# Turning attention weights inside SBUF instead of by way of HBM, in a two-layer attention kernel

## The chip, the cores and the metric

The kernel runs on one core of one Trainium2 chip. The metric is device time in microseconds of that core; the number quoted for a kernel is the median of its runs. A profile is one further execution, recorded instruction by instruction.

## The reference

Two layers of the same shape work on four images of 32 x 32 positions (S = 1024 tokens) with 768 channels. Each layer normalises over 32 groups of channels, runs 12-head attention with head size 64 and decomposed relative position biases, projects the result and adds it to its input. Cut to what matters:

```python
def attention(x, Wqkv, Wproj, bproj, Rh, Rw):          # x: [B, S, 768], after group norm
    q, k, v = split_heads(x @ Wqkv)                     # each [B*12, S, 64]
    rel_h = einsum('bhwc,hkc->bhwk', q.reshape(B*12, 32, 32, 64), Rh)
    rel_w = einsum('bhwc,wkc->bhwk', q.reshape(B*12, 32, 32, 64), Rw)
    bias = (rel_h[..., :, None] + rel_w[..., None, :]).reshape(B*12, S, S)
    attn = softmax(scale * q @ k.T + bias)              # [B*12, S, S]
    return merge_heads(attn @ v) @ Wproj + bproj

x = x + attention(group_norm(x), layer 0)
x = x + attention(group_norm(x), layer 1)               # with a bias on q, k and v
```

All arithmetic is in fp32. The largest piece of data is `attn`: 1024 x 1024 weights for each of 12 heads, 4 images and 2 layers.

## The kernel before

**Units.** Layer and image give eight passes (`images`), each of six head pairs, so there are 48 pairs, numbered `g`; `pair` is the number within its image. A pair is worked through in eight units `n` = 0 to 7 of 128 queries each. The main loop (L566) goes over the 384 units. Scheduling is manual: each engine runs its instructions in the order in which the program writes them.

**Work of a unit**, with the name of the PSUM or SBUF tile that the profile shows. While the loop is at unit n, it issues ahead:
- `biases` (L312) for the unit after next: GpSimd adds the two position terms into `sc` (two instructions, one per head).
- `scores` (L326) for the next unit: TensorE makes `s` = q k (L333; two heads side by side on the upper and lower 64 rows of the array, 512 columns at a time); VectorE adds bias and finds the row extremum in one pass (L342); ScalarE takes the exponential in place (L346). The two banks `s`, one per head, are all that there is: the scores of the next unit need the reductions of this one to be over.
- `turn` (L359) for this unit: VectorE transposes 32 x 32 blocks of the exponentials from `sc` into `tb` (L370).
- `divide` (L351) for the next unit: VectorE's reciprocal (L353), then GpSimd's scaling of `sc` (L356).
- A share of `todo`: the pieces in which TensorE prepares the next pair and projects earlier pairs out. `shares` says how many steps each unit takes.

**Steps of todo.** For the next pair: q in two halves and k in two halves (`project_in`, tile `pj`, L214), six steps each; ScalarE copies half of the contraction out of PSUM (L227 or L229) and VectorE adds the other half (L230). Then two groups of values (`project_values`, tile `pv`, L249), six steps each, with copies by ScalarE and additions by VectorE. From the fourth pair on, also four groups of output projection (`project_out`, tile `o`, L475), three steps each, evacuated by VectorE. `take` runs them in this order. A step of 512 columns costs TensorE 0.86 us: two heads or contraction halves beside each other.

**The tables of positions.** `positions(g, i)` multiplies q by the position tables (tile `tp`, L281); ScalarE copies the result out and sends it to HBM (`tdr`). After both halves `diagonals` (L295) reads it back skewed, with 16 small DMAs on SP's queue, into `rel`. They are put into the lists `early`, `mid` and `later`. In each unit `early` is run and then swapped with `later`: a thing put into `later` runs two units on; one put into `early` after the swap runs one unit on.

**The path of the weights to the value product.** The product needs keys on partitions, the exponentials have queries on partitions. The 32 x 32 block transposes leave each block in its partition group; what is left is a movement of data between partitions. Two units make a quarter of 256 queries. After the second, for each head, SP writes `tb` to HBM (`td`, L373, 1 MiB) and, one or two units later, reads it back in another order into `pt` (`read_back`, L381, 1 MiB). The lists `behind` and `behind2` hold the read until then.

**The value product.** `weigh` (L388) multiplies two quarters by the values into `av` (L399), 256 columns per instruction, two heads in the left and right 64 columns of the array; VectorE copies `av` into `attn` (L408, or L411 with the bias of layer 1). It runs at the end of unit 6 for quarters 0 and 1, and at the end of unit 2 of the next pair for quarters 2 and 3. The last pair's two quarters are done one by one after the loop.

**PSUM**: two tiles of two banks for `s`, two for everything else (`ps_m`).

Of the kernel before, what the change touches and what calls it, by code (L numbers as in the profile page):

```python
# [31 lines left out]
FP = mybir.dt.float32  # L32
# [4 lines left out]
P = 128  # L37
B, HW, C = 4, 32, 768
S = HW * HW
NH, D = 12, 64  # L40
NC = C // P
NT = S // P
# [3 lines left out]
HALF = 512  # L46
LAYERS = 2
NP = NH // 2
# [6 lines left out]
def attention_blocks(ctx: ExitStack, tc: tile.TileContext, a: dict, out: bass.AP):  # L55
    nc = tc.nc
# [8 lines left out]
    vpool = ctx.enter_context(tc.tile_pool(name="v", bufs=3))  # L65
    scpool = ctx.enter_context(tc.tile_pool(name="sc", bufs=6))
    tmppool = ctx.enter_context(tc.tile_pool(name="tmp", bufs=1))
    tbpool = ctx.enter_context(tc.tile_pool(name="tb", bufs=3))
    ptpool = ctx.enter_context(tc.tile_pool(name="pt", bufs=2))
    relpool = ctx.enter_context(tc.tile_pool(name="rel", bufs=2))  # L70
    iopool = ctx.enter_context(tc.tile_pool(name="io", bufs=4))
    small = ctx.enter_context(tc.tile_pool(name="small", bufs=4))
# [11 lines left out]
    NPAIR = NI * NP  # L84
# [33 lines left out]
    for l in range(LAYERS):  # L118
        tab = const.tile([P, 2, 2 * HW], FP, tag=f"tab{l}", name=f"tab{l}")
        nc.gpsimd.memset(tab, 0.0)  # L120
        for i, ax in enumerate("hw"):
            src = a[f"rel{ax}{l}"]
            n = src.shape[1]
# [78 lines left out]
    def project_in(g, which, i):  # L202

        im, pair = divmod(g, NP)
        xn, w = xn_of[im], w_of[g, which]
        cols = slice(i * HALF, (i + 1) * HALF)
        if i == 0:
            tag = "qk"[which]
            qk_of[g, which] = qkpool.tile([P, S], FP, tag=tag, name=f"{tag}_{g}")
        t = ps_m.tile([P, 2, HALF], FP, tag="m", name=f"pj_{g}_{which}_{i}")  # L210
        for c in range(NC):
            for a in range(2):
                rows = slice(a * D, (a + 1) * D)
                nc.tensor.matmul(  # L214
                    t[:, a, :], lhsT=w[rows, c, :], rhs=xn[c][rows, cols],
                    start=(c == 0), stop=(c == NC - 1),
                )
            if c < NC - 1:
                yield True
        to, t = qk_of[g, which], [t[:, a, :] for a in range(2)]  # L220
        if which == 1:
            to = to.rearrange("p (a m) -> p a m", a=4)[:, :, i * P : (i + 1) * P]
            t = [x.rearrange("p (m a) -> p a m", a=4) for x in t]
        else:
            to = to[:, cols]
        if images[im][0] == 0:
            nc.scalar.copy(to, t[0])  # L227
        else:
            nc.scalar.activation(to, t[0], AF.Identity, bias=bqkv[:, which, pair : pair + 1])  # L229
        nc.vector.tensor_tensor(to, t[1], to, ALU.add)  # L230
        if which == 0:
            (later if g else mid).append(lambda: positions(g, i))
        if i == 1 and g + 1 < NPAIR:
            later.append(lambda: load_w(g + 1, which))
        yield True
# [121 lines left out]

    def turn(g, n):

        quarter, j = divmod(n, 2)
        for h in range(2):
            if j == 0:
                tb_of[h] = tbpool.tile([P, HW, 2, HW], FP, tag="tb", name=f"tb_{g}_{n}_{h}")
            tb = tb_of[h]
            nc.vector.transpose(tb[:, :, j, :], sc_of[g, n, h])  # L370
            if j == 1:
                td = dram2.tile([P, S * 2], FP, tag=f"td{h}", name=f"td_{g}_{n}_{h}")
                nc.sync.dma_start(out=td, in_=tb.rearrange("p k n i -> p (k n i)"))  # L373
                (behind if quarter % 2 else behind2).append(
                    lambda queue=None, h=h, td=td: read_back(g, quarter, h, td, queue)
                )

    def read_back(g, quarter, h, td, queue=None):
        pt = ptpool.tile([P, 4, NT, 2 * HW], FP, tag=f"pt{h}", name=f"pt_{g}_{quarter}_{h}")
        pt_of[g, quarter, h] = pt  # L380
        (queue or nc.sync).dma_start(  # L381
            out=pt.rearrange("p r k t -> p r (k t)"),
            in_=td.rearrange("(r j) (a t) -> (j a) r t", r=4, a=4),
        )

    def weigh(g, quarters):

        if quarters[0] == 0:
            attn_of[g] = apool.tile([P, S], FP, tag="attn", name=f"attn_{g}")
        n = len(quarters)
        av = ps_m.tile([P, S], FP, tag="m", name=f"av_{g}_{quarters[0]}")[:, : n * 2 * P]
        for at, quarter in enumerate(quarters):
            for k in range(NT):
                for h in range(2):
                    rows = slice(h * D, (h + 1) * D)
                    nc.tensor.matmul(  # L399
                        av[rows, at * 2 * P : (at + 1) * 2 * P], lhsT=v_of[g][:, k, rows],  # L400
                        rhs=pt_of[g, quarter, h][:, :, k, :], start=(k == 0), stop=(k == NT - 1),
                    )
        at = quarters[0] * 2 * P
        to = attn_of[g][:, at : at + n * 2 * P].rearrange("p (q n r i) -> p q r n i", q=n, n=2, r=4)
        av = av.rearrange("p (q r n i) -> p q r n i", q=n, n=2, r=4)
        im, pair = divmod(g, NP)
        if images[im][0] == 0:
            nc.vector.tensor_copy(to, av)  # L408
        else:
            for q in range(n):  # L410
                nc.vector.tensor_scalar(to[:, q], av[:, q], bqkv[:, 2, pair : pair + 1], None, ALU.add)  # L411

    def cuts(im):
        return [0, NC // 2, NC] if im + 1 < NI else [0, NC // 2, NC - 1, NC]
# [86 lines left out]

    early, mid, later, behind, behind2 = [], [], [], [], []

    def run(todo):
        while todo:  # L510
            todo.pop(0)()
# [30 lines left out]
    with tc.manual_schedule(engines=ENGINES):  # L542
# [23 lines left out]
        for at, (g, n) in enumerate(units):  # L566
            im, pair = divmod(g, NP)
            end = im + 1 == NI
            if n == 0:
                shares = [6, 6, 0, 6, 12, 6, 0, 12]  # L570
                ins = (todo if at == 0 else []) + prepare(g + 1)
                if pair < 3:
                    if at == 0:
                        shares = [12, 6, 0, 6, 12, 6, 0, 0]
                    todo = ins + (put_out(im - 1, 1, range(4 * pair, 4 * pair + 4)) if im else [])
                elif pair < NP - 1:
                    todo = ins + put_out(im, 0, range(4 * pair - 12, 4 * pair - 8))
                    if pair == 3 and not end:
                        stages, apply = norm(im + 1)
                else:  # L580
                    todo = ins + put_out(im, 0, range(8, 12))
                    if end:
                        fetch_last()
                        todo += put_out(im, 1, range(12)) + put_out(im, 2, range(0, 12, 2))
                        shares = [6, 6, 0, 6, 6, 2, 0, 4]
            if (pair, n) in loads and not end:
                load_x(im + 1, loads[pair, n])
            if im + 1 < B:
                if (pair, n) in loads0:
                    load_x(im + 1, loads0[pair, n], loads0[pair, n] + AHEAD)  # L590
                if pair < 3 and n in (1, 3, 5, 6):
                    c, i = divmod(4 * pair + n // 2, 2)
                    x = xn_of[im + 1][c % AHEAD][:, i * HALF : (i + 1) * HALF]
                    later.append(lambda c=c, i=i, x=x: stats(im + 1, (c + AHEAD) % NC, i, x))
            run(early)
            early, later = later, early
            if at + 2 < len(units):
                biases(*units[at + 2])
            if at + 1 < len(units):
                scores(*units[at + 1])  # L600
            run(behind)
            behind, behind2 = behind2, behind
            if pair == 3 and n in stages and not end:
                stages[n]()
            if pair == 4 and n in (2, 4, 6) and not end:
                apply(n // 2 - 1)
            share = shares[n]
            first = 3 if n == NT - 1 else 2 if end and pair == NP - 1 and n in (3, 4) else 0
            first = min(first, share)
            take(todo, first)  # L610
            share -= first
            turn(g, n)
            if at + 1 < len(units):
                divide(*units[at + 1])
            if pair == 4 and n == 7 and not end:
                for chunks in ((3, 4), (5,)):
                    take(todo, 3)
                    share -= 3
                    for c in chunks:
                        apply(c)  # L620
            take(todo, share)
            if n == 6:
                weigh(g, (0, 1))
            elif n == 2 and g:
                weigh(g - 1, (2, 3))
        for read in behind:
            read(nc.scalar)
        take(todo, 12)
        for quarter in (2, 3):
            weigh(NPAIR - 1, (quarter,))  # L630
        todo = put_out(NI - 1, 2, range(1, 12, 2))
        take(todo, len(todo))

# [54 lines left out]
```

## Time and profile before

| | us |
|---|---|
| median of 3 runs | 3504.99 (3502.89 to 3509.22) |
| span of the profiled execution | 3507.0 |
| ScalarE: exponentials L346, 768 | 879.8, of 1147 ns each |
| VectorE: score reductions L342, 768 | 909.8, of 1222 ns |
| VectorE: block transposes L370, 768 | 910.7, of 1222 ns |
| GpSimd: biases L319, 768 | 1890.4, of 2485 ns |
| GpSimd: divisions L356, 768 | 855.1, of 1127 ns |
| TensorE: av L399, 6144 records | 689.1, of 382 ns |
| DMA: 624,857 packets | 1084.54 MB, mean 309 GB/s |
| DMA: td<-tb, 384 of 1 MiB | 5.9 from issue to landing (median) |
| DMA: pt<-td, 384 of 1 MiB | 7.6 from issue to landing (median; those of SP) |

The span is first instruction to last in the profiled execution, 2.0 us above the median of the runs and within their spread. A TensorE instruction in fp32 makes two records, and two instructions on different parts of the array run beside each other; records last longer than the steps between them, since their ends are modelled. So TensorE time is best read as the distance from one group's start to the next one's. The granted TensorE clock is 0.998 on average, with short stretches at half speed at the start, near 123, 133 and 198 us, and at the end. DMA queue q1 (SP) takes 83.4% of the DMA engines' time, q10 (ScalarE) 4.4%.

### The profile page before, as it was taken

Reading aid. Unit: us, or ns where it says so; the run is one execution under the profiler, and the core shown is the slowest. Engines: PE = TensorE matmul, PEld = TensorE weight load, DVE = VectorE, ACT = ScalarE, POOL = GpSimd, SP = SyncE. Lnnn points to the kernel's source line nnn. Section 1 sums busy time; section 2 is a strip of 40 time slices with the busy share of each in tenths; the row PEclk is TensorE's granted clock in tenths of the full one; section 3 lists DMA queues with packets and bytes.
Section 4 is the critical chain, followed back from the end, with each engine's and each line's share of the span. In section 5 each row is a group of like instructions: output and inputs, shape, how many; then the busy total and the mean of one; then the engine's idle time right before and its main releaser. Section 6 shows DMA issues by size and latency. Waiting matters only on the chain.

```text
span 3507.0 us, 55102 instructions
## 1 busy us (share of the span) xinstructions
PE 3462.3 (99%) x21120; PEld 1921.4 (55%) x21120; DVE 2381.1 (68%) x3676; ACT 1227.5 (35%) x2040; POOL 2729.9 (78%) x1546
## 2 busy tenths in 40 slices
PE   6999999999999999999999999999999999999999
PEld 4555555555555555555555555555555555555554
DVE  4666767767677676767767667666666667666666
ACT  2334333333333333333333333333333333333331
POOL 3888887778777787788777788787787778787774
PEclk9999999999999999999999999999999999999999
DMA  4889989999899898898989989899889988898877
GB/s 137 312 308 311 332 293 337 319 316 326 304 329 323 313 316 313 312 324 305 326 305 326 320 292 332 311 331 306 300 327 324 321 298 316 319 322 295 311 275 281
DMA packets 624857, 1084.54 MB, mean 309 GB/s; under 512 B 247120, under 2 KB 310096, under 8 KB 575440
## 3 DMA queue, kind: packets, MB, share of 16 engines
q1 hardware_dynamic: 569008, 1028.29, 83.4%
q10 hardware_dynamic: 55584, 52.72, 4.4%
q8 instruction: 166, 2.72, 0.3%
q14 instruction: 99, 0.81, 0.1%
HBM read 580.59 MB, written 500.27 MB: 308 GB/s over the span
## 4 chain that ended last, share of the span: by engine, by line
PE 97%; DMA 2%; DVE 0%; SPq 0%; issue 0%; ACT 0%; POOL 0%; ACTq 0%; DVEq 0%
PE pj L214 28%; PE s L333 19%; PE av L399 19%; PE o L475 14%; PE pv L249 14%; PE tp L281 3%; DMA tdr<-t 1%; DMA pt<-td 1%; SPq L307 0%; DMA td<-tb 0%; DMA wo<-in_wo 0%; DMA xn<-in_x 0%; DVE st L152 0%; DMA rel<-tdr 0%; DMA per<-mv 0%
## 5 line engine op out<-in xcount | busy, mean ns | idle before, releaser
L319 POOL TENSOR_TENSOR sc<-rel 128x1024 f32<-128x1024 f32 x768 | 1890.4, 2485 | 38.2 <-DMA rel<-tdr 38.2
L356 POOL TENSOR_SCALAR sc<-sc,sm 128x1024 f32<-128x1024 f32 x768 | 855.1, 1127 | 686.1 <-DVE sm L353 669.2
L346 ACT ACTIVATE sc<-sc,sm 128x1024 f32<-128x1024 f32 x768 | 879.8, 1147 | 1370.9 <-DVE sm L342 1368.7
L342 DVE CUSTOM_DVE_ANT_0 sc<-s,sc 128x1024 f32<-128x1024 f32 x768 | 909.8, 1222 | 293.3 <-PE s L333 266.4
L214 PE MATMUL pj<-xn,w 64*128 64x512 f32 x4608 | 1033.5, 591 | 26.8 <-DVE xn L193 25.7
L370 DVE STREAM_TRANSPOSE tb<-sc 128x1024 f32<-128x1024 f32 x768 | 910.7, 1222 | 22.9 <-DMA td<-tb 20.5
L214 PEld LDWEIGHTS pj<-xn,w 64*128 64x128 f32 x4608 | 453.2, 188 | 568.6 <-issue 536.6
L333 PE MATMUL s<-k,q 64*128 64x512 f32 x3072 | 750.1, 598 | 7.0 <-DVE sm L342 6.9
L399 PE MATMUL av<-pt,v 128*64 128x256 f32 x6144 | 689.1, 382 | 6.1 <-DMA pt<-td 6.1
L399 PEld LDWEIGHTS av<-pt,v 128*64 128x64 f32 x6144 | 434.5, 137 | 289.8 <-ACT v L259 35.6
L249 PE MATMUL pv<-wv,xn 64*128 64x256 f32 x4608 | 515.7, 376 | 0.0
L249 PEld LDWEIGHTS pv<-wv,xn 64*128 64x128 f32 x4608 | 448.3, 187 | 90.8 <-issue 30.1
L475 PE MATMUL o<-attn,wo 128*128 128x512 f32 x1080 | 475.8, 597 | 0.2 <-DMA wo<-in_wo 0.2
L333 PEld LDWEIGHTS s<-k,q 64*128 64x128 f32 x3072 | 288.5, 187 | 299.5 <-issue 275.5
L475 PEld LDWEIGHTS o<-attn,wo 128*128 128x128 f32 x1080 | 201.4, 190 | 271.4 <-issue 260.9
L260 DVE TENSOR_TENSOR v<-pv,v 128x256 f32<-128x256 f32 x192 | 81.5, 425 | 277.6 <-ACT v L259 277.6
L259 ACT COPY v<-pv 128x256 f32<-128x256 f32 x192 | 71.5, 372 | 330.7 <-PE pv L249 282.9
L286 ACT COPY t<-tp 128x1024 f32<-128x1024 f32 x96 | 97.2, 1012 | 245.5 <-PE tp L281 148.5
L346 ACT ACTIVATION_READ_ACCUMULATOR sc<-sc,sm 128x1 f32 x768 | 143.6, 187 | 0.0
L230 DVE TENSOR_TENSOR q<-pj,q 128x512 f32<-128x512 f32 x96 | 66.4, 692 | 107.5 <-ACT q L227 56.0
L230 DVE TENSOR_TENSOR k<-pj,k 128x512 f32<-128x512 f32 x96 | 66.4, 692 | 95.5 <-ACT k L227 49.0
L281 PEld LDWEIGHTS tp<-tab,q 64*128 64x128 f32 x1536 | 100.0, 187 | 39.9 <-issue 39.6
(34 smaller groups left out, 787.6 us busy)
## 6 DMA issues: line engine op xcount, KB each, us to landing
td<-tb SPq DMA_DIRECT2D x384, 1024.0 KB, 5.9
pt<-td SPq DMA_DIRECT2D x382, 1024.0 KB, 7.6
tdr<-t ACTq DMA_DIRECT2D x96, 512.0 KB, 6.3
w<-in_wqk SPq DMA_DIRECT2D x96, 384.0 KB, 7.5
rel<-tdr SPq DMA_DIRECT2D x760, 32.0 KB, 2.3
part<-res SPq DMA_DIRECT2D x84, 256.0 KB, 5.5
res<-part SPq DMA_DIRECT2D x84, 256.0 KB, 9.1
wv<-in_wv SPq DMA_DIRECT2D x24, 768.0 KB, 8.7
```

Of the source, the lines that this page charges most:

```text
L214: nc.tensor.matmul(t[:, a, :], lhsT=w[rows, c, :], rhs=xn[c][rows, cols], start=(c == 0), stop=(c == NC - 1),)
L230: nc.vector.tensor_tensor(to, t[1], to, ALU.add)
L249: nc.tensor.matmul(t[:, a, k, :], lhsT=xn[c][rows, (2 * i + k) * P : (2 * i + k + 1) * P], rhs=w[rows, c, :], start=(c == 0), stop=(c == N ...
L281: nc.tensor.matmul(ps[:, h, j, :], lhsT=q[rows, at * P : (at + 1) * P], rhs=tabs[l][rows, :], start=True, stop=True,)
L319: nc.gpsimd.tensor_tensor(sc.rearrange("p (a k) (u l) -> p a (k u) l", a=4, l=8), rel[:, h, 0, n, :].unsqueeze(1).unsqueeze(3).to_broadcas ...
L333: nc.tensor.matmul(ps[h][:, cols], lhsT=q[rows, n * P : (n + 1) * P], rhs=k[rows, cols], start=True, stop=True,)
L342: nc.vector.tensor_tensor_reduce(out=sc, in0=ps[h], in1=sc, scale=-scale, scalar=BIG, op0=ALU.add, op1=ALU.min, accum_out=st[:, 0, h : h + 1],
L346: nc.scalar.activation(sc, sc, AF.Exp, bias=st[:, 0, h : h + 1], scale=-1.0, accum_out=st[:, 1, h : h + 1],)
L356: nc.gpsimd.tensor_scalar(sc, sc, st[:, 2, h : h + 1], 1.0, ALU.mult, ALU.mult)
L370: nc.vector.transpose(tb[:, :, j, :], sc_of[g, n, h])
L399: nc.tensor.matmul(av[rows, at * 2 * P : (at + 1) * 2 * P], lhsT=v_of[g][:, k, rows], rhs=pt_of[g, quarter, h][:, :, k, :], start=(k == 0) ...
L475: nc.tensor.matmul(t, lhsT=wo_of[im, o, c], rhs=attn_of[im * NP + c][:, cols], start=(c == c0), stop=(c == c1 - 1),)
```

## The change

The weights no longer go through HBM. A block b is again 256 queries (two units), but both heads now share one `tb` tile of 2 MiB, and `move` copies it straight into `pt` with 16 DMAs of 128 KiB: for each of the four residues `a` of the destination partitions and each group `r` of 32 source partitions. DMAs with r = 0 and 2 are issued on SP, those with r = 1 and 3 on ScalarE. `move` is run in the unit after the block's second one, after that unit's `scores` are issued, so on ScalarE behind their exponentials. One `pt` tile holds two blocks of both heads, with one buffer; `tb` has two.

`weigh` takes a half (512 queries) at once with 512 columns per instruction. It runs at the end of unit 5 and of unit 1 of the next pair. The shares of `todo` change with it, `positions` of q's first half run one unit earlier, and the list `behind2` is gone. After the loop the last block is moved, what is left of `todo` is done and then the last half is weighed. [...]

```diff
-    tbpool = ctx.enter_context(tc.tile_pool(name="tb", bufs=3))
-    ptpool = ctx.enter_context(tc.tile_pool(name="pt", bufs=2))
+    tbpool = ctx.enter_context(tc.tile_pool(name="tb", bufs=2))
+    ptpool = ctx.enter_context(tc.tile_pool(name="pt", bufs=1))
...
-            (later if g else mid).append(lambda: positions(g, i))
+            (mid if not g else later if i else early).append(lambda: positions(g, i))
...
+        b, j = divmod(n, 2)
+        if j == 0:
+            tb_of[b] = tbpool.tile([P, HW, 2, 2, HW], FP, tag="tb", name=f"tb_{g}_{b}")
+        tb = tb_of[b]
         for h in range(2):
-            if j == 0:
-                tb_of[h] = tbpool.tile([P, HW, 2, HW], FP, tag="tb", name=f"tb_{g}_{n}_{h}")
-            tb = tb_of[h]
-            nc.vector.transpose(tb[:, :, j, :], sc_of[g, n, h])
-            if j == 1:
-                td = dram2.tile([P, S * 2], FP, tag=f"td{h}", name=f"td_{g}_{n}_{h}")
-                nc.sync.dma_start(out=td, in_=tb.rearrange("p k n i -> p (k n i)"))
-                (behind if quarter % 2 else behind2).append(
-                    lambda queue=None, h=h, td=td: read_back(g, quarter, h, td, queue)
+            nc.vector.transpose(tb[:, :, h, j, :], sc_of[g, n, h])
+        if j == 1:
+            behind.append(lambda: move(g, b, tb))
+
+    def move(g, b, tb):
+        half, u = divmod(b, 2)
+        if u == 0:
+            pt_of[g, half] = ptpool.tile(
+                [P, 2, 4, NT * 4 * HW], FP, tag="pt", name=f"pt_{g}_{half}"
+            )
+        pt = pt_of[g, half].rearrange("(j a) u r x -> a j u r x", a=4)
+        src = tb.rearrange("p (a k) h n i -> p a (k h n i)", a=4)
+        for a in range(4):
+            for r in (0, 2, 1, 3):
+                (nc.scalar if r % 2 else nc.sync).dma_start(out=pt[a][:, u, r, :], in_=src[r * HW : (r + 1) * HW, a, :])
+
+    def weigh(g, half):
...
+        for k in range(NT):
+            for h in range(2):
+                rows = slice(h * D, (h + 1) * D)
+                nc.tensor.matmul(
+                    av[rows, :], lhsT=v_of[g][:, k, rows], rhs=pt[:, :, k, h, :],
+                    start=(k == 0), stop=(k == NT - 1),
                 )
...
             if n == 0:
-                shares = [6, 6, 0, 6, 12, 6, 0, 12]
+                shares = [12, 0, 6, 6, 12, 0, 6, 6]
...
                     if at == 0:
-                        shares = [12, 6, 0, 6, 12, 6, 0, 0]
+                        shares = [12, 6, 6, 6, 12, 0, 0, 0]
...
-                        shares = [6, 6, 0, 6, 6, 2, 0, 4]
+                        shares = [6, 0, 6, 5, 4, 0, 5, 2]
...
             run(behind)
-            behind, behind2 = behind2, behind
...
-            first = 3 if n == NT - 1 else 2 if end and pair == NP - 1 and n in (3, 4) else 0
+            first = 0 if n < 6 else 2 if end and pair == NP - 1 else 3
...
-            if n == 6:
-                weigh(g, (0, 1))
-            elif n == 2 and g:
-                weigh(g - 1, (2, 3))
-        for read in behind:
-            read(nc.scalar)
-        take(todo, 12)
-        for quarter in (2, 3):
-            weigh(NPAIR - 1, (quarter,))
+            if n == 5:
+                weigh(g, 0)
+            elif n == 1 and g:
+                weigh(g - 1, 1)
+        run(behind)
+        take(todo, len(todo) * NC)
+        weigh(NPAIR - 1, 1)
...
-    nc = bacc.Bacc("TRN2", target_bir_lowering=False, num_devices=1)
+    nc = bacc.Bacc("TRN2", target_bir_lowering=False, num_devices=1, dynamic_dma_scratch_size=1024)
```

## The prediction

> **What bounds the kernel now.** I read four views: the page's busy times and chain, the waits of TensorE, its timeline over one head pair in mid-run, then ACT and SP at the start, where they show what a DMA issue costs.
>
> ```profile
> PE 3462.3 (99%) x21120; PEld 1921.4 (55%) x21120; DVE 2381.1 (68%) x3676; ACT 1227.5 (35%) x2040; POOL 2729.9 (78%) x1546
> ...
> PE 97%; DMA 2%; DVE 0%; SPq 0%; issue 0%; ACT 0%; POOL 0%; ACTq 0%; DVEq 0%
> ```
>
> TensorE sets the time: 3462.3 of 3507.0 us busy, and the chain is TensorE throughout. DMA is on it for 2%, though the DMA engines are 88% busy: halving their traffic buys nothing by itself.
>
> ```profile
> PE s L333 <- DVE sm L342: 6.9, 6, 1.4
> PE av L399 <- DMA pt<-td: 6.1, 3, 3.0
> ```
>
> Apart from the 25.7 us start these are the only waits of weight, and asking for 270 to 3415 us alone lists none: nothing to win in mid-run by an earlier arrival. Where the named ones lie:
>
> ```profile
> 119.04 0.65 PE L399 MATMUL av<-pt,v 128*64 128x256 f32 x2 [0.74 <-DMA pt<-td]
> 122.66 5.35 PE L399 MATMUL av<-pt,v 128*64 128x256 f32 x30 [2.98 <-DMA pt<-td]
> 127.94 1.99 PE L333 MATMUL s<-k,q 64*128 64x512 f32 x8
> 131.36 3.45 PE L333 MATMUL s<-k,q 64*128 64x512 f32 x7 [1.43 <-DVE sm L342]
> ...
> 3491.42 5.35 PE L399 MATMUL av<-pt,v 128*64 128x256 f32 x30 [2.40 <-DMA pt<-td]
> ```
>
> The first value product, the seams of the first three pairs (131, 197, 262 us), and the last product. Now the timeline, start against start:
>
> ```profile
> 1508.66 5.32 PE L214 MATMUL pj<-xn,w 64*128 64x512 f32 x24
> 1513.81 1.88 PE L333 MATMUL s<-k,q 64*128 64x512 f32 x8
> 1515.53 5.32 PE L214 MATMUL pj<-xn,w 64*128 64x512 f32 x24
> 1520.68 5.35 PE L249 MATMUL pv<-wv,xn 64*128 64x256 f32 x48
> 1525.86 1.88 PE L333 MATMUL s<-k,q 64*128 64x512 f32 x8
> ...
> 1532.76 1.88 PE L333 MATMUL s<-k,q 64*128 64x512 f32 x8
> 1534.57 7.13 PE L399 MATMUL av<-pt,v 128*64 128x256 f32 x64
> 1541.62 1.99 PE L333 MATMUL s<-k,q 64*128 64x512 f32 x8
> 1543.54 10.57 PE L475 MATMUL o<-attn,wo 128*128 128x512 f32 x24
> 1554.04 1.99 PE L333 MATMUL s<-k,q 64*128 64x512 f32 x8
> 1555.86 5.32 PE L214 MATMUL pj<-xn,w 64*128 64x512 f32 x24
> ```
>
> Scores (s) take 1.72 us between projections, 1.81 ahead of av, 1.92 between av and o, 1.82 after o: each change of array shape (64x128, 128x64, 128x128) costs 0.1 us in the scores, and more inside the visiting group.
>
> [...] (two 512-column passes in 5.15/12 = 0.4292 us, two 256-column ones in 5.18/24 = 0.2158). [...] every new copy reads 32 partitions.
>
> **Part by part.** A pair's eight units are n = 0 to 7; Tn is the start of unit n's scores or tables on TensorE.
>
> *Wider products.* A half costs 16 x 0.4292 instead of 32 x 0.2158 us: 0.04 less, 96 halves: -3.8 us. The switches (7.05 - 6.91 = 0.14 inside) stay.
>
> *Shares.* Value products move from n = 2 and 6 to n = 1 and 5, with the same neighbours. But the four output groups of a pair, 12 steps together in n = 7, become 6 in n = 6 and 6 in n = 7 with scores between: one more visit to the 128x128 shape. Price: 0.1 into it, 10.50 - 24 x 0.4292 = 0.20 inside, 0.1 after: 0.40 us. Pairs 3 to 46: 44 x 0.40 = +17.5 us.
>
> *First three pairs* have no output groups, so n = 6 and 7 hold scores alone, where before it was n = 7. Scores then run at VectorE's pace: reductions 2.3, transposes 2.4, reciprocal 0.1, with GpSimd's 7.1 per unit behind. Following unit by unit: s(7) ends 10.6 us after T5, its reductions at 13.2, transposes and reciprocal at 15.6, the next reductions at 18.0, the scores after them at 19.9, against 14.1 for a TensorE that never waits. Loss 5.8; before, some 2.4 (1.43 of wait and the serial halves around it). 3 x 3.4 = +10 us.
>
> *First and last product.* DMAs of two units earlier have landed by then (rel issues end near 100 us, the copies near 108, the product comes near 112), so 0.74 + 2.98 go, and 2.0 of half clock behind them (30 matmuls in 5.28 instead of 3.24): -5.7. At the end, 14 steps (12 us) cover the last copies: -2.4, -1.7 of half clock, +0.5 since both bias additions (0.88) stand before the last outputs: -3.6.
>
> *Copies.* 768 transfers of 1 MiB (805 MB) become 3,072 of 128 KiB (403 MB): -402 MB, worth nothing here. The cost is where they are issued. In units 0, 2, 4 and 6 ACT issues eight directly behind its exponentials, and its copies out of PSUM queue behind them. Nearest row:
>
> ```profile
> 50.53 4.54 ACTq L307 DMA_DIRECT2D rel<-tdr x8
> 55.11 0.59 ACT L227 COPY k<-pj 128x512 f32<-128x512 f32 x1 [7.54 <-DMA rel<-tdr]
> ```
>
> Eight on ACT beside eight on SP: 4.54 us, and the k copy waits. Also
>
> ```profile
> SPq L124 <- DMA xn<-in_x: 5.3, 3, 2.2
> ```
>
> in SP's own waits: tables of positions wait for inputs with which they share no data, so DMAs must wait for the landing of one some eight back. That holds the fifth copy of each engine until the first has landed (2.0 to 3.2 us for those eight). I take 4.8 us per eight, since each carries four times the bytes; bounds 4.2 and 6.
>
> Unit 2 is the tight one. Exponentials end at T2 + 6.65 (tables 1.0, then 5.65 as at 1506.94 to 1512.6), copies are issued until 11.45. The k projection is done at 7.86, so its PSUM copy is 3.6 us late; copy and addition take 1.3 (1514.03 to 1515.33), behind which VectorE has the reductions of n = 4's scores (2.3 + 0.1). They end at T2 + 15.15, plus 0.14 to TensorE, 15.3. The scores of unit 4 want that bank at T4 = T2 + 7.86 + 6.87 = 14.73. TensorE waits 0.57. In unit 4 the exponentials then end near T4 + 7.0, the copies are issued by 11.8 and landed by 14.1 (2.3 each); the product comes at 13.9 plus the 0.57 lost. That just fits. Units 0 and 6 have room: q after 12 us, o without ACT. I take 0.6 us for 47 pairs: +28 us. Bounds: 0 with a block of 4.2 us; 3 us per pair (+140) with 6, where the landing misses the product too.
>
> On SP eight copies follow the 16 rel loads (0.5 to 0.67 each) and end before ACT's. Tables one unit earlier: cost nothing, hidden by TensorE. Fewer tb and pt buffers: a tb half has two units, pt is free once the product ahead of the scores is done: nothing.
>
> **Sum.** -3.8 + 17.5 + 10 - 5.7 - 3.6 + 28 = +42 us on the span of 3507.0. The span stands 2.0 above the median of 3504.99 and inside its runs (3502.89 to 3509.22), so the median goes to about 3546 us.
>
> **Rivals.**
> 1. *The ACT block stays hidden* (block under 4.3 us): no stall in unit 4; +14, 3519 us. For it: ACT is 35% busy and SBUF copies need no HBM read. Against: 0.1 us of margin.
> 2. *Copies land late*: [...] block 6 us, landing after T4 + 15; +90 to +160, around 3620 us. For it: [...] 0.9 us of room in unit 5. [...]
> 3. *Faster*, one mechanism: the output groups' second visit turns out free[...]. Then -3.8 - 5.7 - 3.6 = -13 meets only the first pairs' +10; with that stall also under 4 us the result is 3496 or below. It decides once split and stalls together cost less than 6 us. Against: 0.1 us at each of four kinds of border, the same to 0.01 us throughout mid-run.
> 4. *No change*: split half as dear and no stall, +5, 3510 us.
>
> **Chances.** Forecast (+22 to +90) 0.45, rival 1 (+8 to +22) 0.30, rival 2 0.15, rival 4 0.06, rival 3 0.04. A change under 0.2% (7 us) can't be told from none. So faster 0.04, same 0.06, slower 0.90. Range 3513 to 3605: it leaves out rivals 3 and 4 and the worse half of rival 2.
>
> **What would show it.** In the timeline: two o groups of 12 with scores between, 5.35 each; av 7.02 us instead of 7.05; waits of PE s on DVE sm once per pair near 0.6 us, in the unit behind k's first half; ACT's k copy 3 to 4 us behind its projection; av waiting on tb copies in few or no pairs; no pt wait near 120 and 3491 us; seams of about 6 us in the first three pairs. An average wait over 1.5 us per pair, or one below 0.1, would make the size wrong; an unchanged 10.5 us o group, or a faster kernel, the reasoning.

## The result, and the profile after

| | before | after |
|---|---|---|
| median of the runs, us | 3506.7 (3502.89 to 3509.22, 4 runs) | 3855.89 (3850.55 to 3871.68, 4 runs) |
| ratio, 95% interval | 1 | 1.1003 (1.0979 to 1.1026) |
| span of the profiled execution, us | 3507.0 | 3848.8 |
| mean granted TensorE clock | 0.998 | 0.984 |
| DMA traffic | 1084.54 MB | 681.83 MB |

The kernel became 10% slower; 3546 us, with a range up to 3605, had been forecast. The page of the kernel after: busy times, DMA queues (packets, MB, share of 16 engines' span), copies (issuing queue, count, size, median us from issue to landing).

```profile
PE 3604.8 (94%) x18048; PEld 1770.4 (46%) x18048; DVE 2355.5 (61%) x3676; ACT 1213.8 (32%) x2040; POOL 2713.4 (71%) x1546
...
q1 hardware_dynamic: 385744, 426.45, 40.4%
q10 hardware_dynamic: 128256, 252.05, 23.4%
...
pt<-tb SPq DMA_DIRECT2D x1536, 128.0 KB, 2.7
pt<-tb ACTq DMA_DIRECT2D x1536, 128.0 KB, 3.5
```

The 403 MB less are there, and no engine does more than before. But TensorE, 99% busy before, is 94% busy now: it waits. The waits of TensorE (us in total, times, longest):

```profile
PE tp L281 <- DVE q L230: 72.9, 47, 3.6
PE s L333 <- DVE sm L342: 37.5, 47, 2.3
PE av L391 <- DMA pt<-tb: 32.3, 16, 8.5
PE pj L214 <- DVE xn L193: 30.7, 8, 26.0
PE av L391 <- DVE v L260: 27.1, 22, 2.1
```

Before, mid-run had none. Now the tables (tp) wait for q in 47 pairs, the scores for their reductions in about as many, and the value products for the copies; the profile names v or the reductions ahead of many av as well. In 35 of the 43 pairs 3 to 45 the product of unit 5 starts within 0.8 us of the landing of its last copy, whatever is named; in seven, the fourth pairs of their images, it starts 0.1 to 0.3 us behind the addition of v values. Their copy out of PSUM stood behind ScalarE's block, and the product needs their PSUM tile. TensorE's timeline over one pair (start, length, instruction, in brackets the idle time before it and its releaser):

```profile
1519.60 2.70 PE L333 MATMUL s<-k,q 64*128 64x512 f32 x7 [0.41 <-DVE sm L342]
...
1539.42 9.13 PE L391 MATMUL av<-pt,v 128*64 128x512 f32 x32 [4.61 <-DMA pt<-tb]
1548.48 1.99 PE L333 MATMUL s<-k,q 64*128 64x512 f32 x8
1550.39 5.42 PE L464 MATMUL o<-attn,wo 128*128 128x512 f32 x12
1555.74 1.99 PE L333 MATMUL s<-k,q 64*128 64x512 f32 x8
1557.66 5.42 PE L464 MATMUL o<-attn,wo 128*128 128x512 f32 x12
1563.01 1.99 PE L333 MATMUL s<-k,q 64*128 64x512 f32 x8
1564.83 10.47 PE L214 MATMUL pj<-xn,w 64*128 64x512 f32 x48
1578.38 2.08 PE L281 MATMUL tp<-tab,q 64*128 64x128 f32 x16 [3.08 <-DVE q L230]
```

Three stalls, at the scores of unit 4, the product of unit 5 and the tables behind the q projections of unit 0. The product takes 9.13 us where an undisturbed one takes 7.09: TensorE's granted clock was 0.5 from 1536.7 to 1543.5 us, from within the stall on and over 4.1 us of the product. ScalarE's timeline over the same stretch:

```profile
1509.72 1.14 ACT L346 ACTIVATE sc<-sc,sm 128x1024 f32<-128x1024 f32 x1
1509.93 1.14 ACTq L380 DMA_DIRECT2D pt<-tb  x2
...
1511.10 5.96 ACTq L380 DMA_DIRECT2D pt<-tb  x6
1517.10 0.58 ACT L227 COPY k<-pj 128x512 f32<-128x512 f32 x1 [6.15 <-DMA pt<-tb]
...
1525.94 1.12 ACTq L380 DMA_DIRECT2D pt<-tb  x2
...
1527.10 7.65 ACTq L380 DMA_DIRECT2D pt<-tb  x6
1534.79 0.37 ACT L259 COPY v<-pv 128x256 f32<-128x256 f32 x1 [7.61 <-DMA pt<-tb]
...
1568.39 0.48 ACTq L380 DMA_DIRECT2D pt<-tb  x1
...
1569.67 7.31 ACTq L380 DMA_DIRECT2D pt<-tb  x6
1577.02 1.07 ACT L227 COPY q<-pj 128x512 f32<-128x512 f32 x2 [7.34 <-DMA pt<-tb]
```

Eight copies take ScalarE 7.1 us in unit 2 (1509.93 to 1517.06), 8.8 in unit 4, 8.6 in unit 0; the medians over the pairs are 7.19, 6.80, 6.23 and 7.00 us in units 2, 4, 6 and 0. The copy of k, v or q out of PSUM stands behind the block in units 2, 4 and 0. The forecast counted its block of 4.8 us from the end of the exponentials, but the first two issues mostly go out beside the last exponential. What compares with the 4.8 is the part behind the exponentials: 6.2 us in unit 2 and 5.3 to 5.7 in the others (medians).

Where the 341.8 us of span lie, by unit: mean distance from the start of the scores issued in it to that of the next, pairs 3 to 45, us. The last row is experiment e2, in which ScalarE's half of the copies is left out, so that it shows what the new order of units costs without it.

| unit | 0 | 1 | 2 | 3 | 4 | 5 | 6 | 7 | sum |
|---|---|---|---|---|---|---|---|---|---|
| before | 6.98 | 7.77 | 9.88 | 6.87 | 12.05 | 6.90 | 8.87 | 12.41 | 71.7 |
| after | 15.21 | 10.19 | 6.87 | 7.63 | 12.69 | 11.50 | 7.26 | 7.27 | 78.6 |
| e2 | 13.27 | 9.84 | 6.87 | 6.87 | 12.08 | 8.83 | 7.26 | 7.26 | 72.3 |

Against e2 a pair loses 1.9 us at unit 0 (tables behind q), 0.8 and 0.6 at units 3 and 4 (scores and what follows the k copies), 2.7 at unit 5 and 0.4 at unit 1 (products behind the copies): 6.3 us, in 43 pairs 272. By another count over the whole span, TensorE's idle time by the page (span less busy time) rises from 44.7 to 244.0 us, and its time at half clock from 15 us in 5 stretches to 124 us in 30. If half of that is lost, as in the product above (2.04 us more in 4.1 at half clock), it is 54 more.

### The profile page after: what moved, and what is told of

Its sections match the earlier page's. It is cut to its first block, busy times and chain, and to the rows that moved or that the text cites. A ratio compares the mean times of both kernels' runs of the same rounds, so it can differ in the third digit from the quotient of the medians.

```text
span 3848.8 us, 51901 instructions
## 1 busy us (share of the span) xinstructions
PE 3604.8 (94%) x18048; PEld 1770.4 (46%) x18048; DVE 2355.5 (61%) x3676; ACT 1213.8 (32%) x2040; POOL 2713.4 (71%) x1546
## 2 busy tenths in 40 slices
DMA packets 514263, 681.83 MB, mean 177 GB/s; under 512 B 283984, under 2 KB 346960, under 8 KB 514000
## 5 line engine op out<-in xcount | busy, mean ns | idle before, releaser
L333 PE MATMUL s<-k,q 64*128 64x512 f32 x3072 | 859.4, 618 | 39.1 <-DVE sm L342 37.5
L391 PE MATMUL av<-pt,v 128*64 128x512 f32 x3072 | 702.9, 611 | 85.2 <-DMA pt<-tb 32.3
L249 PE MATMUL pv<-wv,xn 64*128 64x256 f32 x4608 | 548.8, 379 | 0.0
L333 PEld LDWEIGHTS s<-k,q 64*128 64x128 f32 x3072 | 318.2, 191 | 442.9 <-issue 246.6
L249 PEld LDWEIGHTS pv<-wv,xn 64*128 64x128 f32 x4608 | 490.7, 187 | 47.3 <-issue 12.7
L391 PEld LDWEIGHTS av<-pt,v 128*64 128x64 f32 x3072 | 239.4, 141 | 544.5 <-issue 519.8
L464 PE MATMUL o<-attn,wo 128*128 128x512 f32 x1080 | 487.6, 601 | 0.0
L281 PE MATMUL tp<-tab,q 64*128 64x128 f32 x1536 | 115.2, 291 | 72.9 <-DVE q L230 72.9
```

The costliest lines, as they stand in the source:

```text
L249: nc.tensor.matmul(t[:, a, k, :], lhsT=xn[c][rows, (2 * i + k) * P : (2 * i + k + 1) * P], rhs=w[rows, c, :], start=(c == 0), stop=(c == N ...
L281: nc.tensor.matmul(ps[:, h, j, :], lhsT=q[rows, at * P : (at + 1) * P], rhs=tabs[l][rows, :], start=True, stop=True,)
L333: nc.tensor.matmul(ps[h][:, cols], lhsT=q[rows, n * P : (n + 1) * P], rhs=k[rows, cols], start=True, stop=True,)
L391: nc.tensor.matmul(av[rows, :], lhsT=v_of[g][:, k, rows], rhs=pt[:, :, k, h, :], start=(k == 0), stop=(k == NT - 1),)
L464: nc.tensor.matmul(t, lhsT=wo_of[im, o, c], rhs=attn_of[im * NP + c][:, cols], start=(c == c0), stop=(c == c1 - 1),)
```

## Experiments

All are edits of the kernel after; long lines are shown in part. Times without an interval are single runs, beside which the kernel before took 3508 to 3511 us on the same chip. The four runs of after lie 21 us apart, so a difference of that size says nothing.

**Theory**: ScalarE's block, with all that stands behind it. **Rival**: the copies themselves, slow at their source and late for the products.

### e1_all_sp: all copies issued by SP

```diff
-                (nc.scalar if r % 2 else nc.sync).dma_start(
+                nc.sync.dma_start(
```

> All sixteen copies of a block are issued by SP, none by ScalarE; the result is the same. Theory A (ScalarE stands in its eight issues, 6 to 7 us per block, and its PSUM copies behind them come late): the waits of tp on VectorE's q (73 us) and of s on its reductions go; SP needs about 10 us for sixteen issues, so av may wait for copies up to 1 us a half; 3520 to 3640 us. Theory B (the copies themselves are slow and land late, whoever issues them): 3800 us or more, with av waiting on tb copies longer than now. Theory C (order of the units: shares, tables one unit earlier, split output groups): about 3850, the tp waits stay.

Measured: 4002.0 us. The waits of tp are gone, those of av on copies are 185.6 us in 41 products, and more under other names. SP's timeline in unit 4:

```profile
1510.21 7.96 SPq L307 DMA_DIRECT2D rel<-tdr  x16
1518.26 10.35 SPq L380 DMA_DIRECT2D pt<-tb  x16
```

Sixteen issues are 10.1 to 11.5 us on SP (medians of the four blocks), 0.63 to 0.72 each, and in unit 4 they start behind 16 small loads. SP alone did not place 16 copies in the time there was; in after an issue took 0.59 us on SP and 0.61 on ScalarE (medians). The time fits the rival (theory B of the expectation), the vanished waits of tp fit the theory; the run doesn't part them cleanly, since taking the block from ScalarE doubled SP's.

### e2_no_act and e3_tiny_act: ScalarE's copies left out, and made tiny

In e2 ScalarE's eight copies of a block are left out, and the products read the other eight twice. In e3 it issues them with 256 bytes of each row instead of 4 KiB, and the products read as in e2.

```diff
 # e2
+                if r % 2 == 0:
-                    rhs=pt[:, :, k, h, :],
+                    rhs=pt[:, 0:8:2, k, h, :].unsqueeze(2).to_broadcast([P, 4, 2, 2 * HW]),
 # e3, with the same rhs
+                if r % 2:
+                    nc.scalar.dma_start(out=pt[a][:, u, r, : 2 * HW], in_=src[r * HW : (r + 1) * HW, a, : 2 * HW])
```

> Left out: the eight copies that ScalarE issues per block; the value product reads the source groups 0 and 2 twice in place of 1 and 3, so that its columns and instructions stay. Theory A: about 3515 to 3540 us, no tp wait. Theory B: half of the copies' bytes are gone, so about half of the loss, near 3680. Theory C: 3800 or more.

> As the run without ScalarE's copies (the product reads groups 0 and 2 twice), but its eight DMAs are still issued and carry 256 bytes per row instead of 4096. The bytes are those of the run before, the issues those of the changed kernel. Theory A in its issue form (0.6 us per issue plus the wait for a landing some eight back): a block of 5 to 6 us on ScalarE, 3600 to 3800 us. Theory B: like the run without them, near it within 30 us.

Measured: 3548.4 us and 3601.9 us. TensorE's waits in e2:

```profile
PE pj L214 <- DVE xn L193: 31.9, 7, 26.0
PE s L333 <- DVE sm L342: 12.8, 8, 2.3
PE o L465 <- DVE sum L478: 5.7, 5, 2.4
PE av L392 <- DMA pt<-tb: 3.3, 1, 3.3
```

No mid-run wait on q or on copies is left (the 3.3 us stand in the last pair): without ScalarE's half the other half costs nothing, although its packets are as slow as after's (245 ns against 242 on average, for those of 4 KiB). What remains, about 40 us over before, is the price of the new order. Tiny copies add 54 us to it, with ScalarE blocks of 5.3, 6.6, 5.3 and 5.3 us: eight issues cost that here, even for 1/16 of the bytes.

### e4_joined: the four output groups in one unit again

```diff
-                shares = [12, 0, 6, 6, 12, 0, 6, 6]
+                shares = [12, 0, 6, 6, 12, 0, 0, 12]
```

> Only the shares change: all four output groups stand in unit 7 again. My price for the split says 17 us less than the changed kernel (44 x 0.40), 3830 to 3840, if nothing else moves; theory A and B alike say that the waits in units 0, 3, 4 and 5 stay. Theory C says a larger gain, 50 us or more.

Measured: 4108.7 us, 253 slower. Units 6 and 7 take 3.40 and 15.89 us instead of 7.26 and 7.27: 4.8 more for the two, where the split had been priced at 0.4. Unit 6 then holds scores alone, so the next scores ask at once for banks that VectorE still reduces, as in the first three pairs; waits of s on reductions rise to 99 us, and half clock to 387 us. The 17 us less that had been expected did not come. The split costs 0.4 us (5.35 + 1.92 + 5.35 us for the two groups and the scores between in after, 10.50 for the one group and 1.72 for scores elsewhere before), and undoing it costs more.

### e5_src_rows: source rows spread over all partitions

Each copy takes every fourth partition as its source instead of 32 neighbours; sizes, counts and destinations are the same, and the weights reach the products in another order than they should. Every row then also ends in the partition in which it began. The first case of the text below is rival 2's: the source rows make the copies slow.

```diff
-        src = tb.rearrange("p (a k) h n i -> p a (k h n i)", a=4)
+        src = tb.rearrange("(j e) (r k) h n i -> e j r (k h n i)", e=4, r=4)
...
-                in_=src[r * HW : (r + 1) * HW, a, :]
+                in_=src[a][:, r, :]
```

> Left out: the movement between partitions. Each of the sixteen copies keeps its 32 rows of 4 KiB, its queue and its destination, but reads partitions 4j + a, spread over all 128, instead of 32 neighbouring ones; the weights arrive in the wrong order. [...] packets fall towards 170 ns, landings to 2.4 us, ScalarE's block from 7 to about 5.3 us, the time to 3600 to 3680. Theory of concurrency (two queues at once on the same engines, wherever the rows lie): within 30 us of the changed kernel, 3830 to 3880.

Measured: 3652.7 us, 203 less than after. Its page:

```profile
q1 hardware_dynamic: 385744, 426.45, 35.8%
q10 hardware_dynamic: 128256, 252.05, 18.5%
...
pt<-tb SPq DMA_DIRECT2D x1536, 128.0 KB, 2.1
pt<-tb ACTq DMA_DIRECT2D x1536, 128.0 KB, 2.3
```

Same packets, same bytes, less time: 63.8% of 3848.8 us is 2455 us of 16 engines, 54.3% of 3650.9 is 1982; 473 x 16 over the 98,304 packets of the copies makes 77 ns each. The packet records say the same: those of 4 KiB last 242 ns on average after, 168 here (the median is 159 in both). ScalarE's blocks are 5.9, 5.1, 5.2 and 5.0 us. In this order of work the source rows are thus worth the largest part of the loss. The run doesn't show what it is about them: that they lie spread over all partitions, or that no row changes its partition. No other run parts these two.

### e6_swap and e7_no_sp: which copies stand in each other's way

e6 changes the order in which ScalarE takes its two groups of partitions, so that other pairs of groups are read at a time; the first figure of its text is for copies that are slow because of the groups read beside them. e7 leaves SP's copies out, and the products read ScalarE's twice.

```diff
 # e6
-            for r in (0, 2, 1, 3):
+            for r in (0, 2, 3, 1):
 # e7, with rhs=pt[:, 1:8:2, ...] doubled as in e2
+                if r % 2:
```

> ScalarE's order is 3, 1 instead of 1, 3; nothing else. [...] 50 to 150 us less. Otherwise, and also if the queues drift against each other: within 20 us of 3856.

> Left out: the eight copies that SP issues per block; the product reads source groups 1 and 3 twice. ScalarE's eight copies stay whole. Theory of concurrency (ScalarE stands 7 us instead of 5.3 because each of its issues waits for a landing some eight DMAs back, half of which are SP's): block near 5.3, time like that of the run with tiny copies, 3590 to 3630. If the bytes of its own copies hold ScalarE: block near 7, 3750 or more.

Measured: 3874.3 us and 3873.8 us. The order of ScalarE's two groups makes no difference that single runs can show. And leaving out SP's copies gains nothing, though leaving out ScalarE's gained 307 us; neither case expected for e7 came out whole. ScalarE's timeline in e7, units 2, 4 and 6:

```profile
1506.17 5.70 ACTq L381 DMA_DIRECT2D pt<-tb  x6
1511.92 0.58 ACT L227 COPY k<-pj 128x512 f32<-128x512 f32 x1 [7.82 <-DMA pt<-tb]
...
1521.92 3.87 ACTq L381 DMA_DIRECT2D pt<-tb  x6
1525.83 0.37 ACT L259 COPY v<-pv 128x256 f32<-128x256 f32 x1 [3.84 <-DMA pt<-tb]
...
1545.34 9.55 ACTq L381 DMA_DIRECT2D pt<-tb  x6
```

Six issues take 3.87 us in unit 4 but 5.70 in unit 2 and 9.55 in unit 6; the medians of eight are 8.9, 5.0, 9.1 and 5.0 us in units 2, 4, 6 and 0. Units 2 and 6 are those in which SP sends many small DMAs of its own (position loads, rows of the output). TensorE's loss moves to the scores behind the k copies, with 9.60 and 13.83 us in units 3 and 4. The semaphore records of the trace, in which each landing stands, show how SP comes into it: in after eight semaphores serve the DMAs of both engines, 575 or 576 DMAs each. Of 4,605 DMAs 4,597 have one before them on the same semaphore, 4,108 of these five to ten back (median eight), and none is issued before that one has landed, whoever issued it. In the pair shown above, ScalarE's issue at 1533.62 us follows the landing, at 1533.60, of a copy that SP issued at 1526.72. Of ScalarE's 1,536 copies 436 are issued within 0.05 us of such a landing, 204 of these that of a DMA of SP. ScalarE's block is thus not its own: SP's landings lengthen it.

### e8_dve_copies: the copies of q and k out of PSUM by VectorE

```diff
-            nc.scalar.copy(to, t[0])
+            nc.vector.tensor_copy(to, t[0])
...
-            nc.scalar.activation(to, t[0], AF.Identity, bias=bqkv[:, which, pair : pair + 1])
+            nc.vector.tensor_scalar(to, t[0], bqkv[:, which, pair : pair + 1], None, ALU.add)
```

> The first copy of q and k out of PSUM moves from ScalarE to VectorE; all sixteen copies and their queues stay. If TensorE loses its time because these PSUM copies stand behind ScalarE's issues: the waits of tp on q (73 us) and of s on reductions (37 us) and most of the half-clock behind them go, 3650 to 3740; the waits of av stay. If the loss is one of landing alone: 3830 or more.

Measured: 3839.4 us, 16 less than after's median and 11 below its fastest run. TensorE's waits:

```profile
PE av L391 <- DMA pt<-tb: 85.7, 26, 9.1
PE av L391 <- DVE v L260: 51.5, 21, 4.3
PE av L391 <- DVE sm L342: 47.9, 12, 8.0
...
PE s L333 <- DVE sm L342: 14.5, 8, 2.3
```

The waits for q and k behind ScalarE are gone, as they should be (units 0 and 3 are at 13.19 and 6.87 us), and nearly the whole loss stays: units 1 and 5 went to 11.53 and 13.23. TensorE comes to the products earlier and waits there for copies that land no sooner. The landing is a second limit close behind the first. It isn't free of the block, though: in unit 4 ScalarE starts its issues 1.4 us earlier and is through with them at the same time after the unit's start, 13.4 us against 13.3; the last copy lands at 16.2 us against 16.1 (medians).

### e9_eased: 4 of 16 copies on ScalarE

SP takes twelve, and the position loads of unit 4 go behind them.

```diff
-                (nc.scalar if r % 2 else nc.sync).dma_start(
+                (nc.scalar if r == 3 else nc.sync).dma_start(
...
-            later.append(lambda: diagonals(g))
+            (tables if g > 1 else later).append(lambda: diagonals(g))
...
             run(behind)
+            if n == 4:
+                run(tables)
```

> The changed kernel with four of the sixteen copies on ScalarE (r = 3 alone) instead of eight, and with the 16 loads of rel of the next pair issued behind the copies of unit 4 instead of ahead of them. ScalarE then stands about 2.5 to 3.5 us. If the length of that stand decides: tp and s waits go, av waits at most 1 us a half, 3545 to 3620 us. [...] 3780 or more.

Measured: 3709.5 us, ratio to before 1.0573 (1.0554 to 1.0593). ScalarE's blocks are 2.4 to 3.7 us, unit 5 is undisturbed (8.83). Unit 1 is not, with 13.13: SP's twelve issues of unit 0 take 11.3 us, the last ends 14.3 us after the unit's start and lands at 16.7 (medians), where an undisturbed product starts at 14.8 (e2). The time lies between the two cases expected: a shorter stand of ScalarE (up to 3620 us), and copies that are slow whoever issues them (3780 or more). In none of the three ways tried (none, four or eight of 16 on ScalarE) was one unit long enough for the copies.

### e10_room and e11_room2: the kernel before's order, with two units for the copies

The shares and the tables of the kernel before; products of 512 queries at the end of units 6 and 2, one unit later than in the kernel after; copies moved in units 3, 4, 7 and 0, 4 of 16 on ScalarE. In unit 4 SP's share (part 0) goes ahead of the position loads. e11 gives ScalarE 6 of 16 for the copies of unit 0 and 8 in the last pair.

```diff
-                shares = [12, 0, 6, 6, 12, 0, 6, 6]
+                shares = [6, 6, 0, 6, 12, 6, 0, 12]
...
+            if n == 4:
+                move(*behind[0], part=(0,))
             run(early)
...
-            run(behind)
+            if n == 4:
+                move(*behind.pop(0), part=(1,))
+            elif n in (3, 7) or (n == 0 and g):
+                move(*behind.pop(0))
...
-            if n == 5:
+            if n == 6:
                 weigh(g, 0)
-            elif n == 1 and g:
+            elif n == 2 and g:
 # e11, in move: which copies ScalarE issues
+                act = r == 3 or r == 1 and (g + 1 == NPAIR or b == 3 and a < 2)
```

> Built to use what the runs showed: order of units, shares and tables as in the kernel before, products of 512 columns at the end of units 6 and 2, four of sixteen copies on ScalarE, and the copies of the four blocks issued in units 3, 4, 7 and 0, so that each pair of copies has two units or more until its product. [...] no waits in mid-run and 3490 to 3507 us (my prices: -3.8 for the products, -5.7 and -3.6 for first and last). If SP with 48 copies a pair can't keep pace: 3520 or more, with av waits.

> The kernel of e10 with more of the copies on ScalarE where it has time: 6 of 16 instead of 4 for the block that is moved in unit 0, and 8 of 16 for all blocks of the last head pair. Theory (a serial block of about 0.6 us per copy and the landing behind it are what is left): the value products of unit 2, which came up to 0.8 us late in about one pair of four, come on time (-4 us), and the last product comes 7 to 10 us earlier, so 3508 to 3514 us, within 0.2% of the kernel before or just above. Rival (the landing, not the issue, holds the last product[...]): the last product stays near 3500 us after the start and the time at 3520 us or more.

Measured: e10 3524.2 us, ratio 1.0047 (1.0030 to 1.0064); e11 3513.3 us, ratio 1.0017 (1.0010 to 1.0024). TensorE's waits in e11 from 280 to 3415 us, all of them, and from its timeline the last product:

```profile
PE av L393 <- DMA wo<-in_wo: 0.4, 1, 0.4
PE av L393 <- DVE q L230: 0.4, 1, 0.4
PE av L393 <- DMA pt<-tb: 0.3, 1, 0.3
```

```profile
3494.68 8.98 PE L393 MATMUL av<-pt,v 128*64 128x512 f32 x32 [5.40 <-DMA out<-sum]
```

The same 3,072 copies from 32 neighbouring partitions (packets of 246 ns, no faster than after) run beside a TensorE that waits 1.1 us in 3135; in e10, which came out above the 3490 to 3507 us hoped for with copies that do no harm once they have time, it is 7.2 us. These kernels differ from after in the order of work, the time given and ScalarE's share at once, so they don't say which of the three was needed. The scores of the last pair's second unit start at 3417.1 us, 1.0 earlier than before; the last pair then loses 8.3: 3.9 at its first product (2.24 of wait on copies, and half clock), 1.3 at an output that waits for its sum, 3.2 at the last product, which nothing covers. The last product came 8.8 us earlier than in e10, as expected, but its wait (6.32 us there) shrank by only 0.9. The line names another DMA, but the last issues of copies end at 3490.2 us and the last copies land at 3494.5, just ahead of it: landing, and not only issue, holds it. No version tried beats the kernel before.

## Why the prediction was wrong

The direction and the place were right: nothing in mid-run gained by less DMA traffic, and the loss comes through ScalarE's block and, for a small part, through the split output groups (0.40 us per pair). The size missed by 310 us: the block of eight issues was taken too short, and of what stands behind it only one thing was given a price. (The sum's 3504.99 + 42 is 3547, not 3546, which changes nothing.) The runs divide the 349 us between the two medians so:

| step of the chain | time, us | difference |
|---|---|---|
| before | 3507 | |
| e2: the new order, SP's eight copies | 3548 | +41 |
| e3: eight issues on ScalarE | 3602 | +54 |
| e5: their bytes; all sixteen with source rows of e5 | 3653 | +51 |
| after: source of 32 neighbours | 3856 | +203 |

The step to e5 changes two things, and the middle three are single runs. The waits overlap, as e8 shows, so the differences belong to this order of steps.

*Wider products, switches.* Right: the undisturbed product of 512 columns stands 7.02 us from the next scores as forecast, the split groups 5.35 us each with scores of 1.92 between them (medians of after, where scores between k projections take 1.72).

*First pairs, order, end.* Without the block the forecast had +14 us for the new order, and e2 has +40: about 25 of the 310 lie here. The forecast for the first pairs was +10 - 5.7; e2 has +6.7 up to pair 3. From there to pair 46 it has +23.8 where the split and the wider products made +14: 6 of the 10 are waits of projections on the next image's normalised input (31.9 us in 7 places instead of 25.7 in one), all six new ones in unit 0, where 12 steps of q now stand; the rest is open. The end, forecast at -3.6, is +9.1: outputs wait for their sums (5.7 us), and the first product of the last pair waits 3.3 us for its copies and runs at half clock behind that. That 14 steps cover the last copies is right in e2, where the last product doesn't wait, and failed in after, where it waits 4.1 us.

*The block of eight issues.* This is the step that failed. It was taken as 4.8 us behind the exponentials, with 6 as the upper bound, from the eight small loads of the start. Measured there: 6.2 us in unit 2 and 5.3 to 5.7 in the others; from first issue to last 6.2 to 7.2, against 5.3 in three of four units with tiny copies and 5.0 beside a quiet SP (e7, units 4 and 0). The wait that the forecast read off SP's queue is there: no DMA of after is issued before one on the same semaphore has landed, eight back in the median, over both engines (e7). The one that ScalarE's fifth copy has to follow is its own first in 95 of the 192 blocks, as forecast, and one of SP's in the other 97; in half of the blocks it is issued 0.02 us after that landing. The landing that went into the forecast was too short. The forecast had 2.0 to 3.2 us from the small loads and 2.3 for the copies; the medians are 2.7 on SP and 3.5 on ScalarE. With the source rows of e5 they are 2.1 and 2.3, at packets of 168 ns instead of 242. The forecast had copies that land late because of this source in a rival of 0.15, with a block of 6 us that was its author's estimate; e5 shows that the source rows make them late, and no run shows by what. Nor did it count SP's small DMAs, whose landings ScalarE's issues wait for as well (e7). Three things stand behind the block: the scores of unit 4 (by way of k's copy), the tables (by way of q's) and the product of unit 5. The sum priced the first alone.

*Unit 2.* With 6.2 us in place of 4.8 behind the exponentials the forecast's own sum gives 2.0 us of wait at unit 4's scores; units 3 and 4 together lost 1.4 per pair. This was the mechanism that the forecast named, priced at 0.6, and the smaller part of the loss.

*"Units 0 and 6 have room: q after 12 us"* failed for unit 0, with 73 us of waits. Both q copies stand behind the block, which ends 12.2 us after the unit's start. TensorE is through the 12 steps of q at 12.1 and wants the tables next, with a copy and an addition still to come. "Tables one unit earlier: cost nothing" looked at their place on TensorE, not at the copy that they read. It cost 1.9 us per pair.

*"That just fits"* in unit 5 failed by 2.7 us per pair. ScalarE is through with its issues of unit 4 at 13.3 us after the unit's start instead of 11.8 (the exponentials end 0.6 later, and more of the block stands behind them), and the last copy lands at 16.1 instead of 14.1. The product starts at 16.6 (all medians) where it starts at 13.9 in e2.

*The clock.* The sum had no term for it in mid-run, though it read 2.0 us of it off the first product of the kernel before. After has 30 stretches at half clock, of 3.41, 6.83 or 10.24 us (the last one is cut off by the end of the span): 23 of the 30 began in or shortly behind single waits of 1.4 to 3.2 us. The 54 us that this costs more than before are about a sixth of the loss, and in part within the figures by unit above.

*Rivals.* Rival 2, copies that land late because of their source and a block of 6 us, came nearest to what the runs show, and its 3620 us are still too low: it priced the landing, but neither the tables nor the clock. The order in which a queue takes its two groups was no help: swapping it on ScalarE (e6, 3874.3 us) changed nothing that could be seen.

## What to carry to other kernels

Price a DMA that is moved onto a computing engine by its issues, not by its bytes alone: here 0.6 us each, in order with the copies that free PSUM, so that a block of eight (6.2 to 7.2 us in after) stood ahead of what TensorE read next. Then follow every reader behind the block to the tightest one, tables included, and give a stall its stretch of half clock (3.41 us here, behind 23 of 50 waits of 1.4 to 3.2 us). If a later product is possible, give the transfers time rather than speed: one more unit, with the old order of work and fewer copies on ScalarE, took the loss from 349 us to 6, while sharing the copies out otherwise in one unit left 203 us (e9) or made it worse (e1).

## What the hardware showed that was not expected

- DMA waits coupled two issuing engines: the same eight issues took 5.0 us beside a quiet SP and 9.1 us beside an SP with small DMAs in flight (e7).
- With copies within SBUF from 32 neighbouring partitions the packets of 4 KiB took 242 ns on average, from every fourth partition 168 ns, with the same destinations (after, e5). The destinations took every fourth partition in both, so that in e5 no row changed its partition.
- Sixteen issues of 128 KiB took 10.1 to 11.5 us on SP as well (e1), 0.63 to 0.72 each: an issue was no cheaper there than on ScalarE (5.0 us for eight beside a quiet SP, e7).
- A wait of TensorE as short as 1.4 to 3.2 us could be followed by 3.41 us at half clock: 23 of the 30 stretches of after stand at such waits. 27 of its 50 waits of that length were not followed so.
- Leaving half of the copies out gained 307 us when it was ScalarE's half and nothing when it was SP's (e2, e7).
